# Cross-attention with LayerNorm: tiles 28 and 29 are finished one by one, with the centring on VectorE

## The chip, the cores and the metric

The kernel runs on one core of a Trainium2 chip. The metric is the device time of one execution in microseconds, and the median of several runs is compared. The engines are TensorE (PE; its weight loads are PEld), VectorE (DVE), ScalarE (ACT), GpSimd (POOL) and SyncE (SP), which issues DMA transfers. Each engine works through its own instructions in order and waits on semaphores for the others.

## The reference

The inputs are `x` (16 x 256 x 256), a context (16 x 77 x 192), a mask over the context, four weight matrices, and `gamma` and `beta`. There are 8 heads of size 256. Everything is float32.

```python
Q = (img_embed @ Wq).reshape(B, -1, H, D).transpose(0, 2, 1, 3)
K = (sent_embed @ Wk).reshape(B, -1, H, D).transpose(0, 2, 1, 3)
V = (sent_embed @ Wv).reshape(B, -1, H, D).transpose(0, 2, 1, 3)
score = jnp.einsum('bhqd,bhkd->bhqk', Q, K) / math.sqrt(D)
mask = (atten_mask != 0)[:, None, None, :]
score = jnp.where(mask, score, -jnp.inf)
attn = jax.nn.softmax(score, axis=-1)
ctx = jnp.einsum('bhqk,bhkd->bqhd', attn, V).reshape(B, -1, H * D)
out = ctx @ Wo + img_embed
mu = jnp.mean(out, axis=-1, keepdims=True)
var = jnp.var(out, axis=-1, keepdims=True)
return (out - mu) * jax.lax.rsqrt(var + EPS) * gamma + beta
```

What matters here is the last line, the normalisation of each of the 4096 rows of 256 numbers.

## The kernel before

The 4096 rows are 32 tiles of 128 rows, numbered 0 to 31; two tiles make one of the 16 batches (`QT = 2`), and eight tiles share one SBUF tile `xg` and one tile of means and variances `mv`. The weights are folded ahead of the loop: for each batch TensorE makes from the context a matrix for the scores (`pa`, copied to `a`) and one for the product with the attention weights (`pv`, copied to `vw`).

A tile `t` passes through these steps:

- `scores` (L300, TensorE), `shift` (L317, VectorE: minus the score and its minimum, `s` and `top`), `exponential` (L338, ScalarE), `weigh` (L351 and L353 on VectorE, L359 on GpSimd: the division by the sum, into `p`), `turn` (L369, VectorE: a transpose of 32 x 32 blocks, into `pT`);
- `attend` (L381, TensorE): the product of `pT` and `vw`, into the PSUM tile `po`. For most batches `seven` and `add_seven` do it with seven products for eight, for the last ones `attend` does it directly. For the last tile `attend_halves` (L397) makes two PSUM tiles of 128 columns each;
- `finish`: VectorE adds `po` to `x` in `xg` (L497) and takes the statistics of the row (L505, L508). `finish_halves` does it in two halves for tile 31 (L515 to L517);
- `spread` (L526 and L527, ScalarE): one over the standard deviation as Exp(-0.5 Ln(var + eps)), into `rstd`, for one tile or for neighbours at once;
- the normalisation in place in `xg`, in one of three forms. The plain form of `normalise` has two VectorE instructions: `centre` (L547: minus the mean, times gamma) and L566 (times `rstd`, plus beta). The form `aside` computes `less`, minus mean times `rstd` (L537 in `invert`), scales and shifts on ScalarE (L560) and multiplies by gamma and adds beta on GpSimd (L561 and L562). Tile 30 alone has a third form, written out at the end of the kernel: `centre` on VectorE, L1082 on ScalarE (times `rstd`), L1083 on GpSimd (plus beta);
- `store` (L552, SP): one DMA of 128 KB per tile for the last ten tiles.

The schedule is written by hand (`manual_schedule`): each engine carries out its instructions in the order in which the program issues them. The loop over batches, `for b in range(-1, B - 1)`, works in each turn on three neighbouring batches: `new` (scores to `turn`), `now` (`attend`, `finish`) and `old` (normalisation). In its last turn, `b == B - 2`, the new tiles are 30 and 31, the tiles now attended 28 and 29, the old ones 26 and 27. There VectorE's order is: ... statistics of 26 and 27, `turn(30)`, both instructions of tile 27's normalisation, `finish(28)`, `turn(31)`. Tile 26 is normalised `aside`. After the loop come `attend(30)`, `attend_halves(31)`, and then the last four tiles: 28 and 29 `aside` with one `spread` for both and `less` on VectorE, then tile 30 in its own form, and tile 31 with `centre` and L566 on VectorE.

Of the kernel before, what the change touches and what calls it, by code (L numbers as in the profile page):

```python
# [11 lines left out]
AF = mybir.ActivationFunctionType  # L12
ALU = mybir.AluOpType
# [14 lines left out]
def kernel(  # L28
# [13 lines left out]
    nc = tc.nc  # L42
# [4 lines left out]
    NG = B // GB  # L47
    QT = S // P
    NT = B * QT
    GT = GB * QT  # L50
# [56 lines left out]
    bet = const.tile([P, DI], F32, tag="bet", name="bet")  # L107
    xg_of = {}
# [178 lines left out]
    def turn_last(n):  # L287

        blocks = flat(vr[:, 2 * n : 2 * n + 2])
        nc.vector.transpose(blocks, blocks)  # L290
# [75 lines left out]
    def turn(t):  # L366
        p = p_ring[t % 2]
        pT_of[t] = turned.tile([P, NF + 1, NM, BK], F32, tag="pT", name=f"pT_{t}", bufs=4)
        nc.vector.transpose(  # L369
            pT_of[t].rearrange("p n m q -> p m n q"),  # L370
            p.rearrange("p m (n k) -> p m n k", k=BK),
        )
# [122 lines left out]
    def add_product(t):  # L495
        y = xg_of[t // GT][:, t % GT, :]
        nc.vector.tensor_tensor(y, po_of.pop(t), y, ALU.add)  # L497

    def finish(t):
        if t in po_of:  # L500
            add_product(t)
        g, j = t // GT, t % GT
        y = xg_of[g][:, j, :]
        bn = st.tile([P, 6], F32, tag="bn", name=f"bn_{t}")
        nc.vector.bn_stats(bn, y)  # L505
        if j == 0:
            mv_of[g] = st.tile([P, GT, 2], F32, tag="mv", name=f"mv_{g}", bufs=2)
        nc.vector.bn_aggr(mv_of[g][:, j, :], bn)  # L508
# [10 lines left out]
    all_rstd_of, rstd_of, done = {}, {}, []  # L519

    def spread(first, last):

        g, lo, hi = first // GT, first % GT, (last - 1) % GT + 1
        log = st.tile([P, GT], F32, tag="log", name=f"log_{first}")
        rstd = st.tile([P, GT], F32, tag="rstd", name=f"rstd_{first}")
        nc.scalar.activation(log[:, lo:hi], mv_of[g][:, lo:hi, 1], AF.Ln, bias=eps)  # L526
        nc.scalar.activation(rstd[:, lo:hi], log[:, lo:hi], AF.Exp, scale=-0.5)  # L527
        all_rstd_of[first, last] = rstd

    def invert(first, last, aside=(), less_on=nc.gpsimd):  # L530

        g = first // GT
        rstd = all_rstd_of.pop((first, last))
        if aside:
            less = st.tile([P, GT], F32, tag="less", name=f"less_{first}")
            for j in (t % GT for t in aside):
                less_on.tensor_scalar(  # L537
                    less[:, j : j + 1], mv_of[g][:, j, 0:1], rstd[:, j : j + 1], -1.0,
                    ALU.mult, ALU.mult,
                )  # L540
        for t in range(first, last):
            j = slice(t % GT, t % GT + 1)
            rstd_of[t] = rstd[:, j], less[:, j] if aside else None

    def centre(t):
        y = xg_of[t // GT][:, t % GT, :]
        nc.vector.scalar_tensor_tensor(  # L547
            y, y, mv_of[t // GT][:, t % GT, 0:1], gam, ALU.subtract, ALU.mult
        )

    def store(t):
        nc.sync.dma_start(out_rows[:, t, :], xg_of[t // GT][:, t % GT, :])  # L552

    def normalise(t, aside=False, centred=False):

        g, j = t // GT, t % GT
        rstd, less = rstd_of.pop(t)
        y = xg_of[g][:, j, :]
        if aside:
            nc.scalar.activation(y, y, AF.Identity, bias=less, scale=rstd)  # L560
            nc.gpsimd.tensor_tensor(y, y, gam, ALU.mult)  # L561
            nc.gpsimd.tensor_tensor(y, y, bet, ALU.add)  # L562
        else:
            if not centred:
                centre(t)
            nc.vector.scalar_tensor_tensor(y, y, rstd, bet, ALU.mult, ALU.add)  # L566
        if t >= NT - 5 * QT:
            store(t)
            return
        done.append(t)  # L570
        if t ^ 1 in done:
            t |= 1
            j |= 1
            nc.sync.dma_start(
                out_rows[:, t + 1 - QT : t + 1, :], xg_of[g][:, j + 1 - QT : j + 1, :]
            )
# [15 lines left out]
    with tc.tile_pool(name="wonce", bufs=1) as wp:  # L592
        first = -(-GB * S2 // CR)
# [375 lines left out]
    last = NT - 1  # L969
    for b in range(-1, B - 1):  # L970
        old = range(max(b - 1, 0) * QT, b * QT)
        now = range(max(b, 0) * QT, (b + 1) * QT)
        new = range((b + 1) * QT, (b + 2) * QT)
        for t in new if b >= 0 else ():
            scores(t)
        for t in new if b >= 0 else ():
            shift(t)
            if b == B - 2:
                finish(t - 2 * QT)
        while behind:  # L980
            behind.pop(0)()
        g, n = (b + 1) // GB + 1, (b + 1) % GB
        if g < NG and n % 2 == 0:
            load_x(g, n, 2 * QT)
        for m in range(0, 2) if b < 0 else range(b + 2, min(b + 3, B // 2)):
            turn_last(m)
        alone = b + 1 >= B - GB // 2
        works = work_of(b + 1) if alone or n % 2 == 0 else []
        for part_A, _, _ in works:
            part_A()  # L990
        for _, part_B, _ in works:
            part_B()
        if b == B - 2:
            exponential(new[0])
            weigh(new[0])
            turn(new[0])
            spread(old[0], old[1] + 1)
            invert(old[0], old[1] + 1, aside=old[:1])
            normalise(old[1])
            exponential(new[1])  # L1000
            weigh(new[1])
            copy_out(works)
            normalise(old[0], aside=True)
            for t in now:
                attend(t)
            finish(now[0])
            turn(new[1])
            break
        for i, t in enumerate(new if b >= 0 else ()):
            exponential(t)  # L1010
            if old:
                finish(old[i])
            weigh(t)
        ahead = works and not alone
        if old and not ahead:
            spread(old[0], old[-1] + 1)
        if ahead:
            copy_out(works)
            if old:
                spread(old[0], old[-1] + 1)  # L1020
            works = work_of(b + 2, rest_first=True)
            for _, part_B, _ in works:
                part_B()
            for part_A, _, _ in works:
                part_A()
        copy_out(works)
        if b + 1 < NS:
            differences(b + 1)
        if ahead and g < NG:
            load_xT(g, n * QT, (n + 1) * QT, after_pool=True)  # L1030
        if b < NS:
            if now:
                seven(b)
            if old:
                invert(old[0], old[-1] + 1)
                normalise(old[0])
            for t in new:
                turn(t)
            if b < 0:
                for j in range(QT, GT, 2):  # L1040
                    transpose_x(0, j)
                bias_of(GB, B)
            if alone or ahead:
                turn_x_and_normalise(g, n, old)
                if ahead and g < NG:
                    load_xT(g, (n + 1) * QT, (n + 2) * QT)
            else:
                behind.append(partial(turn_x_and_normalise, g, n, old))
            if ahead:
                sums(b + 1)  # L1050
            if now:
                add_seven(b)
            if b + 1 < NS and not ahead:
                sums(b + 1)
            continue
        for t in now:
            attend(t)
        invert(old[0], old[-1] + 1, aside=old[:1])
        normalise(old[0], aside=True)
        turn(new[0])  # L1060
        normalise(old[1])
        turn(new[1])
        for t in now:
            add_product(t)
# [1 line left out]

    attend(last - 1)
    attend_halves(last)
    before = (last - 3, last - 2)
    finish(before[1])  # L1070
    spread(before[0], last - 1)
    invert(before[0], last - 1, aside=before, less_on=nc.vector)
    for t in before:
        normalise(t, aside=True)
    t = last - 1
    finish(t)
    spread(t, last)
    centre(t)
    invert(t, last)
    rstd, _ = rstd_of.pop(t)  # L1080
    y = xg_of[NG - 1][:, t % GT, :]
    nc.scalar.activation(y, y, AF.Identity, scale=rstd)  # L1082
    nc.gpsimd.tensor_tensor(y, y, bet, ALU.add)  # L1083
    store(t)
    finish_halves(last)
    spread(last, NT)
    centre(last)
# [33 lines left out]
```

## Time and profile before

| what | value |
|---|---|
| median of 3 runs | 271.83 us (271.62 to 271.97) |
| profiled execution | 270.92 us |
| its span, first to last instruction | 269.1 us |
| TensorE busy | 262.2 us (97%) |
| VectorE busy | 185.8 us (69%) |
| ScalarE busy | 157.2 us (58%) |
| GpSimd busy | 174.8 us (65%) |
| mean granted TensorE clock | 0.997 |

The page and the views of the trace come from the one profiled execution, and times in them count from the start of its span. A line of a timeline has the start, the length, the engine, the program's line, the instruction, and what it writes and reads; in square brackets stands the idle time of the engine before it and who ended that. "SPq" is the queue of instructions of SP, which issues DMA transfers; the length there is that of the issue, not of the transfer.

### The profile page before, as it was taken

To read this page: it belongs to the slowest core of one execution; us is meant where nothing else is said; L and a number is where in the kernel's file an instruction comes from. 1 tells how busy PE (TensorE), PEld (TensorE's weight loads), DVE (VectorE), ACT (ScalarE), POOL (GpSimd) and SP (SyncE) were. 2 spreads that over 40 slices of the span, in tenths; PEclk is the share of its full clock that TensorE was granted. 3 is DMA by queue.
4 is the path that set the end of the run, shared out by engine and by line. 5 is a ranking of instruction groups with operands and counts; after the bars stand their busy time and mean duration, and the time that the engine had idled before them with its cause. 6 is when DMAs were issued, how large, how long until landed. Compare 5 with 4: busy or idle time off the path is not lost.

```text
span 269.1 us, 14426 instructions
## 1 busy us (share of the span) xinstructions
PE 262.2 (97%) x6090; PEld 190.6 (71%) x6090; DVE 185.8 (69%) x808; ACT 157.2 (58%) x665; POOL 174.8 (65%) x242
## 2 busy tenths in 40 slices
PE   8999999999999999999999999999999999999991
PEld 7566578944984699459945995499669958976661
DVE  1555967493583868665876479647977888799775
ACT  3243336526857465955596458737775594645752
POOL 1042005628399639994799579965997899585445
PEclk9999999999999999999999999999999999999998
DMA  6989999901400220322031301340034010100112
GB/s 192 206 190 218 342 135 167 316 8 40 122 7 2 51 74 2 109 74 61 5 99 50 94 5 44 93 109 4 14 110 122 2 46 5 41 22 22 46 41 78
DMA packets 41616, 22.69 MB, mean 84 GB/s; under 512 B 24064, under 2 KB 40528, under 8 KB 41552
## 3 DMA queue, kind: packets, MB, share of 16 engines
q1 hardware_dynamic: 41168, 20.98, 31.3%
q0 software_dynamic: 384, 0.79, 1.4%
q8 instruction: 48, 0.79, 1.3%
q14 instruction: 16, 0.13, 0.2%
HBM read 17.57 MB, written 4.19 MB: 81 GB/s over the span
## 4 chain that ended last, share of the span: by engine, by line
PE 96%; DMA 2%; DVE 1%; SPq 0%; issue 0%; DVEq 0%
PE ps L300 25%; PE pa L190 13%; PE pv L224 11%; PE po L448 10%; PE pm L448 8%; PE pa L202 6%; PE pv L235 6%; PE po L381 4%; PE pu L767 3%; PE pr L260 2%; PE pgb L828 2%; DMA wq_nat<-in_L_xattn_Wq_dram 2%; PE pw L781 1%; PE phb L844 1%; PE pr L271 1%; PE po L397 1%
## 5 line engine op out<-in xcount | busy, mean ns | idle before, releaser
L338 ACT ACTIVATE e<-s,top 128x77 f32<-128x77 f32 x256 | 85.3, 346 | 44.3 <-DVE top L317 41.2
L300 PE MATMUL ps<-a,xT 128*32 128x154 f32 x2048 | 69.9, 294 | 0.0
L300 PEld LDWEIGHTS ps<-a,xT 128*32 128x32 f32 x2048 | 66.1, 110 | 1.3 <-issue 0.4
L359 POOL TENSOR_TENSOR p<-e,rden 128x512 f32<-128x512 f32 x64 | 47.5, 768 | 29.5 <-DVE rden L353 29.4
L317 DVE CUSTOM_DVE_ANT_0 s<-ps,bias 128x77 f32<-128x77 f32 x256 | 43.5, 232 | 14.3 <-PE ps L300 14.3
L338 ACT ACTIVATION_READ_ACCUMULATOR e<-s,top 128x1 f32 x224 | 41.9, 187 | 0.0
L190 PE MATMUL pa<-cA,gA 128*32 128x308 f32 (+1 forms) x576 | 36.6, 394 | 0.0
L190 PEld LDWEIGHTS pa<-cA,gA 128*32 128x32 f32 x576 | 18.3, 110 | 21.1 <-issue 7.0
L483 POOL TENSOR_TENSOR xg<-xg,m 128x256 f32<-128x256 f32 x39 | 28.7, 737 | 6.6 <-DVE xg L497 4.5
L566 DVE SCALAR_TENSOR_TENSOR xg<-xg,rstd,bet 128x256 f32<-128x256 f32 x27 | 23.1, 854 | 14.1 <-ACT rstd L527 12.7
L224 PE MATMUL pv<-uA,cA 128*32 128x512 f32 x256 | 30.6, 595 | 0.0
L369 DVE STREAM_TRANSPOSE pT<-p 128x640 f32<-128x640 f32 x32 | 25.5, 821 | 3.6 <-POOL p L359 3.5
L412 POOL TENSOR_TENSOR ts<-vw 128x768 f32<-128x768 f32 x13 | 24.0, 1849 | 5.9 <-ACT vw L956 5.9
L956 ACT COPY vw<-pv 128x512 f32<-128x512 f32 x32 | 17.8, 584 | 14.7 <-PE pv L224 8.1
L497 DVE TENSOR_TENSOR xg<-po,xg 128x256 f32<-128x256 f32 x31 | 11.5, 407 | 13.6 <-PE po L448 13.3
L317 DVE DVE_READ_ACCUMULATOR2_ANT top<- 128x1 f32 x256 | 20.8, 81 | 0.0
L202 PE MATMUL pa<-cB,gB 64*32 64x308 f32 (+2 forms) x512 | 20.4, 387 | 0.0
L956 ACT COPY a<-pa 128x308 f32<-128x308 f32 (+1 forms) x56 | 18.9, 396 | 1.9 <-PE pa L190 0.4
L202 PEld LDWEIGHTS pa<-cB,gB 64*32 64x32 f32 (+1 forms) x512 | 11.0, 110 | 11.4 <-issue 6.2
L235 PE MATMUL pv<-uB,cB 64*32 64x512 f32 x256 | 17.3, 597 | 0.0
L547 DVE SCALAR_TENSOR_TENSOR xg<-xg,mv,gam 128x256 f32<-128x256 f32 x28 | 17.0, 606 | 0.1
L224 PEld LDWEIGHTS pv<-uA,cA 128*32 128x32 f32 x256 | 7.5, 109 | 12.8 <-issue 9.9
(120 smaller groups left out, 404.2 us busy)
## 6 DMA issues: line engine op xcount, KB each, us to landing
xT<-in_x_dram SPq DMA_DIRECT2D x52, 64.0 KB, 2.6
xg<-in_x_dram SPq DMA_DIRECT2D x6, 512.0 KB, 4.7
out_dram<-xg SPq DMA_DIRECT2D x11, 256.0 KB, 2.4
wo<-in_L_xattn_Wo_dram SPq DMA_DIRECT2D x4, 512.0 KB, 7.5
wq_blk<-in_L_xattn_Wq_dram SPq DMA_DIRECT2D x12, 128.0 KB, 4.3
out_dram<-xg SPq DMA_DIRECT2D x10, 128.0 KB, 1.7
wk_blk<-in_L_xattn_Wk_dram SPq DMA_DIRECT2D x12, 96.0 KB, 4.0
xg<-in_x_dram SPq DMA_DIRECT2D x1, 1024.0 KB, 8.6
```

Source lines behind the costliest of these rows:

```text
L190: nc.tensor.matmul(flat(o[i * BK : (i + 1) * BK]), gA[:, h, cols(dc, i)], flat(cA[:, batches, :]), start=not rest_first and n in opening, ...
L202: nc.tensor.matmul(flat(banks[j + k][i * BK : (i + wide) * BK]), gB[half(k), h // 2, dc * P + i * BK : dc * P + (i + wide) * BK], flat(cB[ ...
L224: nc.tensor.matmul(pv[k][i * BK : (i + 1) * BK], cA[:, b, k * BK : (k + 1) * BK], uA[:, parts, :, i], start=not rest_first, stop=rest_first,)
L235: nc.tensor.matmul(pv[k][i * BK : (i + 1) * BK], cB[half(k), b, k * BK : (k + 1) * BK], uB[half(k), parts, :, i], start=rest_first, stop=n ...
L300: nc.tensor.matmul(ps[m // 2][i * BK : (i + 1) * BK, m % 2 * 2 * S2 : (m % 2 + 1) * 2 * S2], xT_of[g][:, j * NM + m, dc], flat(a_of[g][:, ...
L317: nc.vector.tensor_tensor_reduce(s[:, h], ps[a][:, k * S2 : (k + 1) * S2], bias[:, b, :], scale=-1.0, scalar=FAR, op0=ALU.add, op1=ALU.min ...
L338: nc.scalar.activation(e[:, h], s[:, h], AF.Exp, bias=top[:, one], scale=-1.0, accum_out=den[:, one] if summed_by_act(t) else None,)
L359: nc.gpsimd.tensor_tensor(part, e_mh[:, :, :, keys], rden_mh.unsqueeze(3).to_broadcast(list(part.shape)), ALU.mult,)
L369: nc.vector.transpose(pT_of[t].rearrange("p n m q -> p m n q"), p.rearrange("p m (n k) -> p m n k", k=BK),)
L448: nc.tensor.matmul(out[i * BK : (i + 1) * BK], weight[:, i], moving, start=first and n == 0, stop=final and n == len(terms) - 1,)
L483: nc.gpsimd.tensor_tensor(to, to, what, ALU.add)
L956: nc.scalar.copy(dst, src)
```

## The change

Tiles 28 and 29 are normalised in the form that tile 30 had: `centre` on VectorE, scaling by `rstd` on ScalarE, the addition of beta on GpSimd. The three instructions, the `spread` ahead of them and the store are now one function, `scale_and_store`. Each tile has its own `spread`. Tile 28's `centre` is issued in the loop's last turn between `finish(28)` and `turn(31)`, and its `scale_and_store` after `turn(31)`. Tile 29's steps come after the loop, ahead of those of tile 30, which are what they were. The two L537 on VectorE, the two L560 on ScalarE, and two L561 and two L562 on GpSimd fall away. Tile 26 keeps the form `aside`.

```diff
-    def invert(first, last, aside=(), less_on=nc.gpsimd):
+    def invert(first, last, aside=()):
...
-                less_on.tensor_scalar(
+                nc.gpsimd.tensor_scalar(
...
+    def scale_and_store(t):
+
+        spread(t, t + 1)
+        invert(t, t + 1)
+        rstd, _ = rstd_of.pop(t)
+        y = xg_of[t // GT][:, t % GT, :]
+        nc.scalar.activation(y, y, AF.Identity, scale=rstd)
+        nc.gpsimd.tensor_tensor(y, y, bet, ALU.add)
+        store(t)
...
             for t in now:
                 attend(t)
             finish(now[0])
+            centre(now[0])
             turn(new[1])
+            scale_and_store(now[0])
             break
...
     attend(last - 1)
     attend_halves(last)
-    before = (last - 3, last - 2)
-    finish(before[1])
-    spread(before[0], last - 1)
-    invert(before[0], last - 1, aside=before, less_on=nc.vector)
-    for t in before:
-        normalise(t, aside=True)
-    t = last - 1
-    finish(t)
-    spread(t, last)
-    centre(t)
-    invert(t, last)
-    rstd, _ = rstd_of.pop(t)
-    y = xg_of[NG - 1][:, t % GT, :]
-    nc.scalar.activation(y, y, AF.Identity, scale=rstd)
-    nc.gpsimd.tensor_tensor(y, y, bet, ALU.add)
-    store(t)
+    for t in (last - 2, last - 1):
+        finish(t)
+        centre(t)
+        scale_and_store(t)
     finish_halves(last)
     spread(last, NT)
     centre(last)
```

## The prediction

> **What bounds the kernel now.** First the page's busy line and the chain by line: TensorE is busy almost throughout, so only work behind its last matmul can move the end. Then the same chain in order of time (start, length, what), its last pieces:
>
> ```profile
> PE 262.2 (97%) x6090; PEld 190.6 (71%) x6090; DVE 185.8 (69%) x808; ACT 157.2 (58%) x665; POOL 174.8 (65%) x242
> ```
> ```profile
> 261.37 2.23 PE po L397 x80
> ...
> 264.52 0.92 DVE xg L547
> ...
> 265.53 0.76 DVE xg L566
> ```
>
> TensorE's last products (tile 31, two halves) end at 263.60. Then VectorE alone carries the end: adds and statistics of tile 31, the centring L547 and the last scaling L566, done at 266.29. The change touches nothing that TensorE does, so I look only at the last 12 us. The timeline of VectorE, then GpSimd, then the stores (start, length, instruction):
>
> ```profile
> 258.04 0.18 DVE L508 BATCH_NORM_AGGREGATE mv<-bn 128x2 f32<-128x6 f32 x1
> 258.40 0.85 DVE L369 STREAM_TRANSPOSE pT<-p 128x640 f32<-128x640 f32 x1 [0.18 <-POOL p L359]
> ...
> 260.98 0.34 DVE L537 TENSOR_SCALAR less<-mv,rstd 128x1 f32<-128x1 f32 x2 [0.60 <-ACT rstd L527]
> 261.44 0.42 DVE L497 TENSOR_TENSOR xg<-po,xg 128x256 f32<-128x256 f32 x1
> ...
> 262.57 0.48 DVE L547 SCALAR_TENSOR_TENSOR xg<-xg,mv,gam 128x256 f32<-128x256 f32 x1
> ```
> ```profile
> 258.00 0.37 POOL L359 TENSOR_TENSOR p<-e,rden 128x104 f32<-128x104 f32 x1
> 258.32 0.74 POOL L561 TENSOR_TENSOR xg<-xg,gam 128x256 f32<-128x256 f32 x1
> ...
> 264.42 0.72 POOL L562 TENSOR_TENSOR xg<-xg,bet 128x256 f32<-128x256 f32 x1
> 265.10 0.91 POOL L1083 TENSOR_TENSOR xg<-xg,bet 128x256 f32<-128x256 f32 x1
> ```
> ```profile
> 266.03 0.33 SPq L552 DMA_DIRECT2D out_dram<-xg  x1
> 266.45 0.38 SPq L552 DMA_DIRECT2D out_dram<-xg  x1
> ```
>
> The same centring L547 takes 0.48 at 262.57 and 0.91 at 264.52. In the second case GpSimd's beta add of tile 29 runs from 264.42 to 265.14, and the centring ends 0.28 after it. The last L566 also meets GpSimd (tile 30's beta add, to 266.01) and again ends 0.28 after it: 0.76 instead of the 0.48 that the same form takes at 256.26 beside an idle GpSimd. So GpSimd, 1.5 us behind with two gamma multiplies, stretches the two instructions that end the kernel. It costs once more: tile 30's store goes out only at 266.03, and tile 31's, whose data is there at 266.29, has to follow it, at 266.45.
>
> Stream transposes, statistics and adds that read PSUM show no such stretch: L369 at 258.40 takes its usual 0.85 beside GpSimd.
>
> **The change, part by part, on the clock of this trace.**
>
> *VectorE, tile 28.* Statistics end at 258.22. A centring now stands ahead of the transpose of tile 31. L547 follows the L508 of tile 30 by 0.03 (262.54 to 262.57), so it starts at 258.26. GpSimd is then in L359 until 258.37, 0.11 on; an L566 that met an L359 with 0.12 left (102.76) took 0.48. VectorE can start the next instruction 0.08 before such a centring ends (L547 ends 263.06, L515 starts 262.98). So the transpose goes from 258.40 to 258.68. Queued behind it: the add, statistics and centring of tile 29, the add of tile 30; and TensorE waits for the transpose, but only from 261.19 (first half of tile 31), where before it was ready at 259.25 and now at 259.53. That delay is covered by TensorE's 1.6 us of tile 29 and 30 products that remain; without them it would be 0.28.
>
> *VectorE, tile 29.* From the transpose the old pitches hold: 0.88, add 259.56, 0.46, statistics 260.02, 0.46, L508 260.48 to 260.66, centring 260.70. The two L537 go away (0.34 busy and 0.60 of wait ahead). GpSimd runs tile 28's beta add then (below) until 260.85, 0.15 on: no stretch by more than a few hundredths (L547 at 102.22, 0.14 left: 0.43). It ends at 261.15 and VectorE is free at 261.07. Tile 30's add can't start before its product: 261.44, as now. So two centrings (2 x about 0.46) take the place of the L537 and its wait, and 0.37 is left over. From 261.44 to 263.59 VectorE has no slack against TensorE (L515 starts at 263.62, 0.02 after the product), so what exceeded this 0.37 would go to the end in full.
>
> *ScalarE.* One Ln and one Exp for two tiles become two of each: one more 0.29 + 0.20. L526 takes the same 0.29 for 128x1 as for 128x2. They stand in idle time (2.29 us before 260.42). Tile 28: Ln 258.26, Exp 258.59 to 258.79, then scaling without bias as L1082 (0.51, against 0.60 for L560 now): 258.83 to 259.34. Tile 29: Ln 260.70, Exp to 261.22, scaling 261.27 to 261.78. Tile 30 unchanged: 263.15 to 263.66.
>
> *GpSimd.* Two gamma multiplies (0.74 and 0.73) go. Tile 26's multiply waits for the centring (0.93 as L562 at 262.72 instead of 0.74), its beta add ends about 260.07, then come tile 28's 260.11 to 260.85, tile 29's 261.85 to 262.59 (0.02 into tile 30's centring, harmless), tile 30's 263.73 to 264.46. GpSimd is idle when the last centring starts at 264.52.
>
> *The end.* Centring of tile 31: 264.52 to about 264.96. The last L566 then waits for ScalarE's Exp, 265.04, unchanged: start 265.09, 0.48, done 265.57 against 266.29: **0.72**. Stores on SP, in the same order: 28 at 260.88 instead of 263.68, 29 at 262.62 instead of 265.17, 30 at 264.49, 31 at 265.60, with nothing in front of it, against 266.45: another **0.13**. The four DMAs stay 128 KB each; the median to landing is 1.7. From 266.45 and 269.1 the last store has 2.65 to the span's end; in company it may land a few hundredths later than alone, for which I take **0.05**.
>
> Sum: 0.72 + 0.13 + 0.05 = **0.90** off the span of 269.1, so 268.2. The profiled execution took 270.92 in all (1.82 around the span), and the runs' median, 271.83, is 0.91 above that; the difference is taken off the median: **270.9**.
>
> **A rule against a row.** The Trainium skill, "SBUF — State Buffer", section "SBUF: two separate sides", says that GpSimd and a VectorE instruction with two SBUF inputs contend for a port pair: who starts first holds it for the whole instruction and the other "fully blocks". That speaks against adding two such centrings. By the rule, tile 28's centring would run in full after 258.37, to 258.85, 0.12 later than by the row, still inside the 0.37: the sum stays 0.90. Blocked instructions in the trace end 0.28 after GpSimd, not 0.43 to 0.48; I take the row. More matters who is first: VectorE asks at 258.26, GpSimd's next (L561) starts at 258.32, so by the rule VectorE goes next. The rows are split:
>
> ```profile
> 197.32 1.37 POOL L359 TENSOR_TENSOR p<-e,rden 128x104 f32<-128x104 f32 x2
> 197.61 1.37 DVE L566 SCALAR_TENSOR_TENSOR xg<-xg,rstd,bet 128x256 f32<-128x256 f32 x1 [1.16 <-ACT rstd L527]
> ```
> ```profile
> 102.76 0.48 DVE L566 SCALAR_TENSOR_TENSOR xg<-xg,rstd,bet 128x256 f32<-128x256 f32 x1
> ```
>
> At 197.61 VectorE was some 0.04 ahead of the second L359 (197.65) and still lost, staying 1.37; at 102.76 it was 0.08 ahead and won. Here it is 0.06 to 0.07 ahead, nearer the winner.
>
> **Rivals.**
> *(B) The centring of tile 28 loses to tile 26's gamma multiply.* It ends 0.28 after 259.06, at 259.34, 0.60 later. Tile 30's add slips to 261.64, its centring then meets tile 29's beta add (about 0.1 more): VectorE runs 0.30 late at tile 31. Saved: 0.90 - 0.30 = 0.60; 271.2.
>
> *(C) Slower: the centrings of 28, 29 and 30 all start just behind a GpSimd add.* Each tile's beta add follows its own scaling by one tile, the same period as VectorE's next centring, so a bad phase could repeat. The price of one is 0.55 (0.99 at 164.18 against 0.44). 0.60 + 0.55 + 0.55 less the cover of 0.37 is 1.33 late, and minus 0.90 leaves 0.43: 272.3. It decides from a lateness of 0.90, so two collisions are not enough; my timeline has at most one. Against it: the beta adds of 28 and 29 end 0.15 and 0.02 into the next centring.
>
> *(D) No change.* The end would have to hang on something besides the last store. For it: the span runs on for 2.65 after the store's issue, mostly outside named work. Against it: SP's own waits end with 0.9 for the landing of the stores, and GpSimd, the other late engine, finishes sooner too. 271.8.
>
> **How the numbers follow.** My forecast has 0.60, B 0.17, D 0.10, C 0.13. About 0.2% (0.54 us) is what a measurement of this kernel can tell from no change. The forecast (0.90 saved) is faster; B (0.60) straddles the bound, 0.09 faster and 0.08 same; D is same; C slower. I move 0.02 from faster to same for the spread of the runs (271.62 to 271.97). Faster 0.67, same 0.20, slower 0.13. The likeliest's own range is 270.6 to 271.1; with B and part of D the range goes to 271.7, leaving out C and some 0.06 at both edges.
>
> **What would show it.** Right: the two last VectorE instructions at about 0.44 and 0.48, GpSimd idle from about 264.5, tile 31's store alone at about 265.6, the span near 268.2, TensorE's end where it was. B shows as a centring of about 1.1 near 258.3. C shows as three centrings near 1.0 and tile 31's first add well after TensorE. D shows both last instructions short and the span unchanged. The prediction fails if TensorE waits for tile 31's transpose, or if ScalarE's scaling of tile 28 comes late because Ln waits for more than its own tile's statistics.

## The result, and the profile after

The changed kernel took 270.47 us (median of 6 runs, 269.91 to 270.98) beside 271.75 for the kernel before (6 runs). The ratio is 0.9949, with a 95% interval of 0.9931 to 0.9966: faster by 1.4 us, between 0.9 and 1.9 (the two medians differ by 1.28). The six runs of before include the three on which the prediction was based. The prediction was 270.9, with a range of 270.6 to 271.7. The direction was right and the time lies outside the range, below it.

The profile looks contradictory at first. The profiled execution of the changed kernel took 270.98 us with a span of 269.2, and that of before 270.92 with 269.1. The chain in order of time (start, length, what) resolves it. Here are its last pieces in the changed kernel:

```profile
262.34 2.23 PE po L397 x80
...
264.59 0.30 DVE xg L515
...
265.48 0.50 DVE xg L547
...
266.07 0.48 DVE xg L576
```

L576 is what L566 was; the lines behind the new function have moved by ten. TensorE's last products started at 262.34 instead of 261.37, so this execution reached them 0.97 us later. From there it was quicker: the last centring takes 0.50 instead of 0.92 and the last scaling 0.48 instead of 0.76. From here on "tail" is the time from the end of TensorE's last product to the end of the span. That end is read from TensorE's timeline, whose last line is in the kernel before and then in the changed one:

```profile
263.15 0.40 PE L397 MATMUL po<-vr,pT 128*32 128x128 f32 x8
```
```profile
264.12 0.40 PE L397 MATMUL po<-vr,pT 128*32 128x128 f32 x8
```

So it is 263.55 before; the chain, from which the prediction read 263.60, counts 0.05 more. The two traces side by side:

| | before | after |
|---|---|---|
| TensorE's last product ends | 263.55 | 264.52 |
| last VectorE instruction ends, after that | 2.74 | 2.04 |
| tile 31's store is issued, after that | 2.90 | 2.06 |
| tail | 5.58 | 4.67 |

The tail is 0.91 us shorter; the prediction's sum was 0.90. VectorE's timeline of the changed kernel, around the two new centrings:

```profile
259.23 0.48 DVE L547 SCALAR_TENSOR_TENSOR xg<-xg,mv,gam 128x256 f32<-128x256 f32 x1
259.63 0.84 DVE L369 STREAM_TRANSPOSE pT<-p 128x640 f32<-128x640 f32 x1
...
261.49 0.60 DVE L547 SCALAR_TENSOR_TENSOR xg<-xg,mv,gam 128x256 f32<-128x256 f32 x1
262.40 0.42 DVE L497 TENSOR_TENSOR xg<-po,xg 128x256 f32<-128x256 f32 x1 [0.32 <-PE po L381]
```

The first centring goes ahead of the transpose and is not stretched. After the second, VectorE still waits 0.32 us for TensorE, so both are covered. GpSimd and the stores in the same execution:

```profile
259.29 1.01 POOL L571 TENSOR_TENSOR xg<-xg,gam 128x256 f32<-128x256 f32 x1
260.38 0.74 POOL L572 TENSOR_TENSOR xg<-xg,bet 128x256 f32<-128x256 f32 x1
261.07 0.73 POOL L561 TENSOR_TENSOR xg<-xg,bet 128x256 f32<-128x256 f32 x1
...
264.71 0.72 POOL L561 TENSOR_TENSOR xg<-xg,bet 128x256 f32<-128x256 f32 x1 [1.21 <-ACT xg L560]
```
```profile
265.45 0.33 SPq L552 DMA_DIRECT2D out_dram<-xg  x1
266.58 0.33 SPq L552 DMA_DIRECT2D out_dram<-xg  x1
```

Tile 30's beta add (264.71) now begins 0.08 after ScalarE's scaling ends (264.63) and is over at 265.43, before the last centring starts at 265.48. Tile 30's store leaves 1.13 us ahead of tile 31's, where it was 0.42.

So the size is the one that the prediction gave, and the instructions that became shorter are the ones that it named. What did not fit was the total: 1.3 to 1.4 measured against 0.9 in the tail. The experiments ask first whether the rest is real, and then whether the gain really has the cause that the prediction names.

### The profile page after: what moved, and what is told of

The parts are those of the page before. It is cut to its first block, busy times and chain, and to the rows that moved or that the text cites. A ratio compares the mean times of both kernels' runs of the same rounds, so it can differ in the third digit from the quotient of the medians.

```text
span 269.2 us, 14427 instructions
## 1 busy us (share of the span) xinstructions
PE 262.9 (98%) x6090; PEld 194.3 (72%) x6090; DVE 185.2 (69%) x808; ACT 157.7 (59%) x667; POOL 173.2 (64%) x240
## 4 chain that ended last, share of the span: by engine, by line
PE 93%; DMA 3%; DVE 1%; SPq 1%; issue 0%; DVEq 0%
PE ps L300 25%; PE pa L190 12%; PE pv L224 11%; PE po L448 11%; PE pm L448 8%; PE pa L202 6%; PE pv L235 6%; PE po L381 4%; PE pu L777 3%; PE pr L260 2%; PE pgb L838 2%; DMA c_sb<-in_ctx_dram 2%; DMA wk_blk<-in_L_xattn_Wk_dram 2%; PE pw L791 1%; PE phb L854 1%; PE pr L271 1%
## 5 line engine op out<-in xcount | busy, mean ns | idle before, releaser
L190 PEld LDWEIGHTS pa<-cA,gA 128*32 128x32 f32 x576 | 19.0, 110 | 20.4 <-issue 6.7
L576 DVE SCALAR_TENSOR_TENSOR xg<-xg,rstd,bet 128x256 f32<-128x256 f32 x27 | 22.2, 821 | 14.7 <-ACT rstd L527 13.3
```

The costliest lines, as they stand in the source:

```text
L190: nc.tensor.matmul(flat(o[i * BK : (i + 1) * BK]), gA[:, h, cols(dc, i)], flat(cA[:, batches, :]), start=not rest_first and n in opening, ...
```

## The experiments

In all of them the tail is read from the profile, where it repeats within 0.02 us (two profiles of the kernel before, three of the changed one). The ratio is that of the whole time to the kernel before on the same chip.

| kernel | TensorE ends | last VectorE end after it | tail | ratio (95% interval) |
|---|---|---|---|---|
| before | 263.55 | 2.74 | 5.58 | |
| e10_before_again | 264.49 | 2.72 | 5.57 | 1.0002 (0.9990 to 1.0014) |
| after | 264.52 | 2.04 | 4.67 | 0.9949 (0.9931 to 0.9966) |
| e1_after_again | 263.96 | 2.04 | 4.69 | 0.9960 (0.9948 to 0.9972) |
| e11_after_third | 263.60 | 2.04 | 4.68 | 0.9969 (0.9957 to 0.9981) |
| e2_no_gamma | 263.94 | 2.46 | 5.11 | 0.9982 (0.9971 to 0.9992) |
| e3_aside_alone | 264.10 | 2.04 | 4.67 | 0.9957 (0.9940 to 0.9973) |
| e4_gamma_twice | 264.26 | 2.47 | 5.12 | 0.9982 (0.9969 to 0.9996) |
| e9_no_beta29 | 264.56 | 2.04 | 4.68 | 0.9970 (0.9955 to 0.9985) |
| e6_centre_after_turn | 264.54 | 2.37 | 5.01 | 0.9983 (0.9966 to 0.9999) |
| e8_more_vector | 264.13 | 2.19 | 4.83 | 0.9968 (0.9952 to 0.9983) |
| e7_store30_on_act | 263.55 | 2.72 | 5.53 | 0.9986 (0.9971 to 1.0001) |

### How large is the gain: the two kernels again

No edit: the changed kernel a second and a third time, and the kernel before against itself.

> The changed kernel once more, to size its gain. Theory T (all of the gain lies behind TensorE's last product; what was measured beyond it is scatter of the time at which TensorE gets there): from TensorE's end to the span's end 4.67 us against 5.59 before, and in the total 0.9 us below before, within 0.3. Rival R1 (a further part comes systematically from ahead of TensorE's end, since the instruction streams differ): the same tail, and again 1.3 to 1.4 us in the total.

> The kernel before, unchanged, measured against itself. Theory T (TensorE reaches its last product at a different time in each execution, and nothing behind it varies): 5.58 us behind TensorE's end, within 0.03, whatever the time of that end (263.5 to 264.6 so far), and a ratio whose interval holds 1. Rival R6 (the profiled execution of before was unusual behind TensorE's end too): a tail of 5.7 to 6.0 us, which would give the change more than 0.91 in the mean.

> The changed kernel for a third time, beside the kernel before measured against itself on the same chip. Theory T: 4.67 us behind TensorE's end and a ratio near 0.9966 (0.91 of 271.5). Rival R1 (a further systematic part from ahead of TensorE's end): 0.995, as in the first comparison.

Before against itself gave 271.50 (12 runs) beside 271.37 (17 runs), a ratio of 1.0002. Its second profile has TensorE's end 0.94 us later than the first and the same tail, 5.57. The chain of that second execution, with both stretched instructions again:

```profile
262.30 2.23 PE po L397 x80
...
264.55 0.30 DVE xg L515
...
265.45 0.91 DVE xg L547
...
266.45 0.76 DVE xg L566
```

The changed kernel's two repetitions gave 270.51 (11 runs) beside 271.52 (29 runs), and 270.41 (6 runs) beside 271.37 (17 runs): 1.0 us faster by the medians each time. Theory T expected a ratio of 0.9966, and both intervals hold it; the 0.995 of rival R1 lies inside the second's interval at its edge and outside the third's. The first comparison's 1.4 was high because its six runs of before were: 271.75, where the later sets of 12 to 31 runs, on two chips, have medians of 271.37 to 271.52, while the changed kernel's three medians agree within 0.1. Why those six were high is not shown. R6 falls, and so does R1 with its 1.3 to 1.4; a tenth or two of a microsecond more than 0.91 can't be told by these runs.

The time at which TensorE finishes is what scatters. Over the twelve profiles it ends between 263.55 and 264.56, and the profile of before that the prediction used is the earliest, together with that of e7_store30_on_act. All of the difference has arisen by 86 us into the span. From there to TensorE's last product each trace keeps its distance to the first one within 0.02: the changed kernel is 0.97 us behind throughout. The two programs differ only at the end, so the change moves nothing of TensorE's work. A part of the scatter is a pause of TensorE at 74 us, in which it waits for nothing that the profile shows. The timeline of TensorE in the first execution of before, and then in the second:

```profile
73.76 0.62 PE L448 MATMUL po<-vw,ss 128*32 128x128 f32 x16
```
```profile
74.08 0.39 PE L448 MATMUL po<-vw,ss 128*32 128x128 f32 x4
74.68 0.52 PE L448 MATMUL po<-vw,ss 128*32 128x128 f32 x10 [0.21 <-issue]
```

The sixteen products run in one stretch in the first and stop between 74.08 and 74.68 in the second. Where this pause and the other steps (most of them in the loading stage, up to 43 us) come from is not shown.

### Which part of the change does it: less work on GpSimd, or an earlier start

The change does two things at once. It takes two multiplies off GpSimd, and it lets tile 28 begin as soon as its own statistics are there. Three kernels have one of these without the other.

Without the multiplies in the old form (gamma is not applied to tiles 28 and 29):

```diff
             nc.scalar.activation(y, y, AF.Identity, bias=less, scale=rstd)
-            nc.gpsimd.tensor_tensor(y, y, gam, ALU.mult)
+            if t < NT - 4:
+                nc.gpsimd.tensor_tensor(y, y, gam, ALU.mult)
             nc.gpsimd.tensor_tensor(y, y, bet, ALU.add)
```

> The kernel before, in which GpSimd's multiplication by gamma is left out for tiles 28 and 29 (so that gamma is not applied there); all else as before, with one Ln and Exp for both tiles and the L537 on VectorE. Theory T1 (GpSimd is late by the two multiplies, and being on time is worth the whole gain, however it is reached): tile 30's beta add starts 0.07 after ScalarE's scaling and the last two VectorE instructions take about 0.44 and 0.48: 0.9 us shorter behind TensorE's end. Rival R2 (the separate, earlier finish of tile 28 is what counts): not more than half of it, below 0.45.

The old form, each tile by itself:

```diff
+    def aside_alone(t):
+        spread(t, t + 1)
+        invert(t, t + 1, aside=(t,), less_on=nc.vector)
+        normalise(t, aside=True)
...
             finish(now[0])
             turn(new[1])
+            aside_alone(now[0])
             break
...
-    finish(before[1])
-    spread(before[0], last - 1)
-    invert(before[0], last - 1, aside=before, less_on=nc.vector)
-    for t in before:
-        normalise(t, aside=True)
+    finish(last - 2)
+    aside_alone(last - 2)
```

> The kernel before, with its old form for tiles 28 and 29 (two instructions on GpSimd each, the mean and scale on ScalarE), but each tile by itself: tile 28's Ln, Exp, L537 and the rest are issued in the loop's last turn, tile 29's after the loop. Theory T1: with a start 1.7 us earlier GpSimd has caught up when tile 30 comes, although it does all its multiplies: 0.8 us shorter behind TensorE's end (0.1 lost where tile 30's centring meets the multiply of tile 29). Rival R3 (GpSimd's amount of work has to fall): 0 to 0.3.

The changed kernel with the multiplies put back (in `scale_and_store`):

```diff
         nc.scalar.activation(y, y, AF.Identity, scale=rstd)
+        if t < NT - 2:
+            nc.gpsimd.tensor_tensor(y, y, gam, ALU.mult)
         nc.gpsimd.tensor_tensor(y, y, bet, ALU.add)
```

> The changed kernel with the two gamma multiplies put back on GpSimd for tiles 28 and 29 (gamma is applied twice there). Theory T1: GpSimd, started early by tile 28, is through with tile 29 at about 0.2 us ahead of tile 30's scaling: 0.85 to 0.9 us shorter than before behind TensorE's end, so next to nothing is given back. Rival R3: GpSimd is late again and the last two VectorE instructions take 0.8 to 0.9 each; the tail is within 0.3 of before.

e3_aside_alone has the whole gain: a tail of 4.67, though GpSimd does all its multiplies. GpSimd's timeline there, with tile 29's multiply and beta add and then tile 30's beta add, and below it VectorE's centring of tile 30:

```profile
262.46 0.73 POOL L561 TENSOR_TENSOR xg<-xg,gam 128x256 f32<-128x256 f32 x1 [0.31 <-ACT xg L560]
263.27 0.93 POOL L562 TENSOR_TENSOR xg<-xg,bet 128x256 f32<-128x256 f32 x1
264.29 0.72 POOL L1086 TENSOR_TENSOR xg<-xg,bet 128x256 f32<-128x256 f32 x1
```
```profile
263.13 0.48 DVE L547 SCALAR_TENSOR_TENSOR xg<-xg,mv,gam 128x256 f32<-128x256 f32 x1
```

GpSimd is through with tile 30 at 265.01, ahead of the last centring at 265.07. Even the 0.1 that I expected to lose was not lost, since tile 30's centring came only 0.06 before the end of the multiply, went ahead of the beta add and took 0.48. So R3 falls: the amount of work on GpSimd need not shrink.

The other two give half: 5.11 and 5.12. In both, GpSimd is in time for the end and the last two VectorE instructions take 0.48 to 0.49 each, near the 0.44 and 0.48 of T1; but T1's number of 0.9 was wrong, and R2's "below 0.45" was missed narrowly, with 0.47 and 0.46. What was stretched is one instruction, tile 30's centring. VectorE, then GpSimd, in e2_no_gamma:

```profile
262.96 1.04 DVE L547 SCALAR_TENSOR_TENSOR xg<-xg,mv,gam 128x256 f32<-128x256 f32 x1
```
```profile
262.98 0.74 POOL L563 TENSOR_TENSOR xg<-xg,bet 128x256 f32<-128x256 f32 x1
```

and in e4_gamma_twice:

```profile
263.28 1.05 DVE L547 SCALAR_TENSOR_TENSOR xg<-xg,mv,gam 128x256 f32<-128x256 f32 x1
```
```profile
263.32 0.73 POOL L563 TENSOR_TENSOR xg<-xg,bet 128x256 f32<-128x256 f32 x1
```

VectorE started 0.02 and 0.04 ahead of tile 29's beta add and still had to wait for all of it. That is the mechanism of rival B, at another tile. To see whether this one meeting is the whole loss, that beta add was left out as well:

```diff
             if t < NT - 4:
                 nc.gpsimd.tensor_tensor(y, y, gam, ALU.mult)
-            nc.gpsimd.tensor_tensor(y, y, bet, ALU.add)
+            if t != NT - 3:
+                nc.gpsimd.tensor_tensor(y, y, bet, ALU.add)
```

> The kernel without gamma multiplies for tiles 28 and 29 in the old form (5.11 us behind TensorE's end), in which tile 29's beta add on GpSimd is left out as well. If the 0.44 that this kernel missed is the collision of tile 30's centring (1.04 us) with that one add, the centring takes 0.49 and the tail is 4.67, 0.91 shorter than before. If it is something else, above all the shared Ln and Exp and the two L537 on VectorE, the tail stays near 5.1.

```profile
263.58 0.48 DVE L547 SCALAR_TENSOR_TENSOR xg<-xg,mv,gam 128x256 f32<-128x256 f32 x1
```

The centring takes 0.48 and the tail is 4.68. The 0.43 was this meeting and nothing else; the shared Ln and Exp and the two L537 cost nothing at the end. This kernel, with less work on GpSimd, has the whole gain without an earlier start, as e3_aside_alone has it with an earlier start and all the work. What the two share is that GpSimd is out of the way when VectorE centres tiles 30 and 31 and scales tile 31.

### The cover ahead of tile 30's add

Tile 28's centring behind the transpose:

```diff
-            centre(now[0])
             turn(new[1])
+            centre(now[0])
             scale_and_store(now[0])
```

> The changed kernel with tile 28's centring behind the transpose of tile 31 instead of ahead of it. Theory T2 (what VectorE loses to GpSimd in tiles 28 to 30 comes off the gain once it exceeds the 0.3 to 0.4 us of cover ahead of tile 30's add): the centring now starts just behind tile 26's beta add, takes about 0.98 instead of 0.48, tile 30's add starts about 0.3 late, tile 30's centring meets tile 29's beta add (0.59): 5.05 us behind TensorE's end, 0.55 shorter than before and 0.38 longer than the change. Rival R4 (order does not matter, VectorE catches up while it waits for TensorE): 4.67.

The tail is 5.01, against 5.05 expected. VectorE's three centrings of tiles 28 to 30, then GpSimd's beta adds of tiles 26, 28 and 29:

```profile
260.15 0.98 DVE L547 SCALAR_TENSOR_TENSOR xg<-xg,mv,gam 128x256 f32<-128x256 f32 x1
...
262.18 0.63 DVE L547 SCALAR_TENSOR_TENSOR xg<-xg,mv,gam 128x256 f32<-128x256 f32 x1
...
263.86 0.65 DVE L547 SCALAR_TENSOR_TENSOR xg<-xg,mv,gam 128x256 f32<-128x256 f32 x1
```
```profile
260.11 0.74 POOL L572 TENSOR_TENSOR xg<-xg,bet 128x256 f32<-128x256 f32 x1
261.80 0.73 POOL L561 TENSOR_TENSOR xg<-xg,bet 128x256 f32<-128x256 f32 x1 [0.95 <-ACT xg L560]
263.49 0.73 POOL L561 TENSOR_TENSOR xg<-xg,bet 128x256 f32<-128x256 f32 x1 [0.96 <-ACT xg L560]
```

All three centrings meet an add. This is rival C's pattern, but with smaller losses: only the first meets its add from the start, the other two come in when it is about half over. It gives back 0.34 of the 0.91. R4 (order does not matter) falls.

Two more statistics instructions on VectorE for tile 29 in the changed kernel, their results unused (`EXTRA` is 2):

```diff
         finish(t)
+        for i in range(EXTRA if t == last - 2 else 0):
+            bn = st.tile([P, 6], F32, tag="bn", name=f"bn_more_{i}")
+            nc.vector.bn_stats(bn, xg_of[t // GT][:, t % GT, :])
         centre(t)
```

> The changed kernel with two more statistics instructions on VectorE for tile 29 (their results are not used), 0.92 us in all, ahead of tile 29's centring. Theory T2: the first 0.55 of it is covered (0.39 of idle time ahead of tile 30's add, 0.16 since the later centring no longer meets GpSimd), tile 30's add starts 0.37 late, its centring meets tile 29's beta add for another 0.09: 5.13 us behind TensorE's end. Rival R4: the wait for TensorE absorbs it, 4.67. Rival R5 (there is no cover): 5.6.

The tail is 4.83: neither rival, and 0.30 less than T2 expected. VectorE's timeline of the two, then of the centrings of tiles 29 and 30:

```profile
260.99 0.72 DVE L1086 BATCH_NORM_STATS2 bn_more<-xg 128x6 f32<-128x256 f32 x2
261.74 0.48 DVE L548 SCALAR_TENSOR_TENSOR xg<-xg,mv,gam 128x256 f32<-128x256 f32 x1
...
263.27 0.65 DVE L548 SCALAR_TENSOR_TENSOR xg<-xg,mv,gam 128x256 f32<-128x256 f32 x1
```

Two sizes were off. The two statistics moved the centring by about 0.63 (261.74, where 0.22 after the start of the last instruction ahead of them, at 260.89, would be 261.11), not by 0.92: the first starts 0.10 after that instruction, which takes 0.18, and the two together take 0.72. And VectorE catches up a little when it is late, since the second half's add no longer waits for TensorE and starts 0.21 behind the first half's statistics instead of 0.33. With 0.63 in place of 0.92, tile 30's add is 0.13 late on the changed kernel's clock; the meeting with tile 29's beta add costs 0.16 more (0.65 for 0.48), and 0.13 of it is caught up: 0.16, as measured. So 0.50 of the delay is absorbed ahead of tile 30's add (0.39 of it the cover, the rest because tile 29's centring, now later, takes 0.48 and not 0.60), and 0.13 more at the wait for tile 31's second half. What exceeds both goes to the end.

### The queue of stores

Tile 30's store of the kernel before on ScalarE's queue, behind the Exp of tile 31:

```diff
     nc.gpsimd.tensor_tensor(y, y, bet, ALU.add)
-    store(t)
...
     invert(last, NT)
+    nc.scalar.dma_start(out_rows[:, t, :], xg_of[NG - 1][:, t % GT, :])
     normalise(last, centred=True)
```

> The kernel before with tile 30's store issued on ScalarE's queue, so that tile 31's store on SP has nothing ahead of it; all else as before. By the prediction's term for the queue: the last store is issued 0.03 behind the last VectorE instruction instead of 0.17, and the tail is 0.14 shorter, 5.44 us. Rival: the two transfers share the way out anyway, and the tail stays at 5.58.

Tile 31's store was issued 0.15 us earlier (2.75 after TensorE's end instead of 2.90), but the tail is only 0.05 shorter, 5.53: from that issue to the end of the span it is 2.78, not 2.68. The issues at the end of this kernel (the last column is the time to landing):

```profile
out_dram<-xg ACTq DMA_DIRECT2D x1, 128.0 KB, 1.8
out_dram<-xg SPq DMA_DIRECT2D x1, 128.0 KB, 1.9
```

Alone, such a store lands after 1.7, as the last one of the changed kernel does. Here the two, 0.28 us apart, took longer. So 0.10 of the 0.15 is lost again in the landing: the rival is nearer here. In the change, the store of tile 30 itself comes early, and there the queue's 0.14 and the landing's 0.07 (from the last issue to the end of the span 2.61 instead of 2.68) are both gained.

The ratio of this kernel, 0.9986, has an interval that holds 1. Its ten runs have a median 0.41 below that of before, 271.03 against 271.44, of which only 0.05 is in the tail: either ten runs can be that far off, or something that the tail doesn't show has a part in it; the runs don't say which.

## Why the prediction was right about the mechanism and wrong about the time

**The sum.** 0.72 for the last two VectorE instructions, 0.13 for the queue and 0.05 for the landing. Measured: 0.70, 0.14 and 0.07, together 0.91, as in the tail. The split between queue and landing could not have been had one without the other, as e7_store30_on_act shows; the sum holds.

**The steps of the two centrings.** On the old clock (0.97 subtracted) tile 28's started at 258.26, as predicted, and took 0.48. Tile 29's started at 260.52 instead of 260.70, and so met more of tile 28's beta add: 0.60 instead of 0.45. The 0.18 comes from a misread line, "the old pitches hold: 0.88". In the kernel before, tile 29's add follows the transpose (258.40) by 0.88, but it had waited for TensorE's product:

```profile
258.60 0.61 PE L381 MATMUL po<-vr,pT 128*32 128x256 f32 x8
```
```profile
259.28 0.42 DVE L497 TENSOR_TENSOR xg<-po,xg 128x256 f32<-128x256 f32 x1
```

The product ends at 259.21, and the add starts 0.07 later, as the adds of tiles 28 and 30 do after their products. In the changed kernel the product is there in time and the add starts 0.76 after the transpose; the step behind it is another 0.04 shorter, and the transpose itself was 0.02 early. The earlier start changed nothing, since the end of a stretched centring hangs on GpSimd: tile 28's beta add ends at 261.80 in the changed kernel and the centring 0.29 later, as at the two stretched instructions of the kernel before. It ended at 261.12 on the old clock, against 261.15 predicted. The cover of 0.37 was 0.39. Nothing of the stretch reached the end.

**"No slack".** The prediction has VectorE without slack from 261.44 to 263.59, so that what exceeded the cover would go to the end in full. That is wrong by 0.12 to 0.13. The add of tile 31's second half at 263.62 had itself waited for its product; VectorE, 0.21 behind the start of the statistics ahead of it where it doesn't wait (e8_more_vector), would have been ready at 263.50. In e2_no_gamma and e4_gamma_twice tile 30's centring took 0.56 and 0.57 longer and the tail grew by 0.44 and 0.45. The forecast did not use this slack, but the prices of B and C are too high by it.

**Rival B.** It did not happen for tile 28, but it was close, and that it did not was luck in part: the margin was a hundredth of a microsecond (see the last section). The centring asked 0.065 to 0.070 us ahead of GpSimd's next instruction in the profiles of the changed kernel and those that keep its order; e2_no_gamma and e4_gamma_twice lost with 0.02 and 0.04. The price of losing at tile 30 was measured there at 0.43 to 0.45. The 0.30 that I had worked out for a loss at tile 28 was not measured.

**Rivals C and D.** C's pattern exists (e6_centre_after_turn), with an end 0.34 late and not 1.33, as two of the three meetings are short and 0.13 is caught up. D is refuted by the tail.

**The step that failed** is the last of the sum: "the runs' median, 271.83, is 0.91 above that; the difference is taken off the median". The difference was right, 0.91 in the tail, and the median was not a good base. It came from three runs, 271.62 to 271.97, whose closeness I took for the spread of this kernel. Single runs of the same kernel later went from 270.82 to 272.77, with medians of 271.37 to 271.52. So the base was some 0.3 too high. From 271.5, the same 0.90 gives 270.6, and the changed kernel's medians were 270.41 to 270.51, with single runs from 269.91 to 270.98; the 0.1 to 0.2 that is left can't be told from that scatter. The lower edge of the range, 270.6, left 0.3 for an error of the base, which the base alone used up. A hint was in sight: the profiled execution lay 0.91 below the median of the three runs, which showed that single executions differ by more than those three did.

**What is attributed.** Five profiles of the two kernels show 0.91 of the gain behind TensorE's end, and from 86 us to that end TensorE keeps its pace in both. The total of about 1.0 may hold 0.1 more from the first 86 us; there the kernel before scatters by as much as 0.94 against itself, so it is not told from chance. That the 0.91 comes from GpSimd being on time and not from the amount of its work is shown by e3_aside_alone, which has all the work, and from the other side by e9_no_beta29, which has the old start.

## What to carry to other kernels

Where two engines that stretch each other share the end of a kernel, count when each of them starts, not only how much it does: here an earlier start of one tile, with all multiplies kept, gave the whole 0.91, and leaving out the two multiplies without it half of that. Read a gain of a few tenths of a per cent from the stretch in which it must arise (here from the last matmul to the end, which repeats within 0.02 us) and take the total's base from many runs, since the start of the kernel scatters by a microsecond. What an instruction adds depends on what stands around it: the aggregate starts 0.46 after the statistics that it reads, yet two more statistics added 0.63 and not 0.92; and the 0.88 from a transpose to the next start held a wait, without which it was 0.76.

## What the runs showed of the hardware that was not expected

Who goes first where VectorE and GpSimd block each other is decided by about 0.06 us. In the twelve traces, 13 times a VectorE instruction with two operands in SBUF started while a GpSimd instruction was still running and 0.002 to 0.054 us ahead of GpSimd's next one: it lost every time and waited for that one too (twelve of these are one place of the program, near 198 us, once in each trace; the other is tile 30's centring in e2_no_gamma). With a lead of 0.065 or more it won every time. Where GpSimd's last instruction had already ended, leads of 0.047 and more won and one of 0.037 (e4_gamma_twice) lost. In the prediction I had two cases, 0.04 and 0.08, and placed 0.065 nearer the winner, which was right by a hundredth of a microsecond, and so by luck. The Trainium skill's rule in "SBUF — State Buffer", "SBUF: two separate sides", that whoever starts first gets the pair, holds by these rows only if VectorE's start is counted 0.04 to 0.06 us after the one that the profile shows.

Two stores of 128 KB issued 0.28 us apart on two queues (e7_store30_on_act) landed after 1.8 and 1.9 us, against 1.7 alone.
